# Layer 1's second product in seven block products instead of eight, with temporaries of several stages in shared buffers

## The chip, the cores and the metric

The kernel runs on one core of a Trainium2 chip. The metric is the time of one launch in device microseconds (us). Runs of one kernel on one chip agree within some 0.4%; every comparison is made with runs of the kernel before on the same chip in the same session.

## The reference, cut to what matters

Four graph layers follow one another on x of 128 batches x 128 nodes x 256 features, all in fp32. Each has a residual and a layer norm. The change touches layer 1:

```python
def _slconv(x, adj, S, W):
    support = jnp.einsum('bnf,fh->bnh', x, W)
    return jnp.einsum('nm,bmh->bnh', adj * S, support)

h = relu(_slconv(x, adj, S, W1))     # 256 -> 512
h = relu(_slconv(h, adj, S, W2))     # 512 -> 1024: the "second product"
return _slconv(h, adj, S, W3)        # 1024 -> 256
```

Layer 0 is attention over 512 edges (scores, a softmax by segments, a gather and a scatter through DRAM); layer 2 multiplies three mixed copies of x with three weights; layer 3 has two batch norms.

## The kernel before

A *quad* is a group of four batches; there are 32. Turn k of the loop works on several quads at once: layer 2 of quad k-1 (`stage_e`), the second product of quad k (`second`), values and queries of quad k+3 (`values_in`, `values`), the first part of layer 3 of quad k-1 (`stage_f`, `hidden`), the end of layer 0 for quad k+1 (`stage_a`), the third product of quad k, and the start of layer 1 for quad k+1 (`mix1`, `first`, `mix2`). An engine's instructions in the order of the source are called its *list* here, and in this case the order counts. Line numbers (L339) are those of the kernel; they shift by edits.

```python
def mix2(k, i):                       # mixing of the hidden features of batch i over the nodes
    pm = ps("pm2").rearrange("p (c n) -> p c n", n=N)
    for c in range(K1):               # K1 = 4
        nc.tensor.matmul(pm[:, c, :], s.h1[i][:, c * P:(c + 1) * P], wt_t, start=True, stop=True)
    nc.vector.tensor_copy(s.m2[:, :, i, :], pm)                                   # L330

def second(k, f):                     # f = 0..7, 128 of the 1024 outputs each
    ph = ps("ph2")
    for c in range(K1):
        nc.tensor.matmul(ph, w2_sb[:, c, f * P:(f + 1) * P],
                         s.m2[:, c].rearrange("p b n -> p (b n)"),
                         start=(c == 0), stop=(c == K1 - 1))                      # L339
    ...
    nc.scalar.activation(h.rearrange("p b n -> p (b n)"), ph, AF.Relu)            # L342

# in the loop; e is the quad two turns ahead, b the next one, g three ahead
    for f in range(K2):               # K2 = 8
        second(c, f)
        if first_one and f == 0:
            attention(b); scatter(b)
        if f % 2 == 0 and has_e:
            score(e, f // 2)          # three VectorE instructions, 3.65 us
        if f % 2 and has_b:
            by_row(b, f // 2)         # ScalarE copy of the scattered attention table
    if has_g and not first_one:
        values_in(g)                  # TensorE transposes x into pt, VectorE copies pt to xt
    if has_a:
        stage_f(a)                    # TensorE: pa
    ...                               # then values(g, 0): pq needs xt
```

## Time and profile before

| | before |
|---|---|
| median of three runs | 3413.97 us (3408.93 to 3415.3) |
| span of the profiled run, mean granted clock | 3411.7 us, 0.990 |
| TensorE busy | 98% |
| VectorE, ScalarE busy | 51%, 30% |
| one steady turn of the loop | 93.72 us |
| half-clock stretches in the steady turns | none |

The busy shares say which engine is full; the timeline says whether it ever waits; the view of waits adds up by line what TensorE waited for. In the kernel before that last view holds nothing in the loop above this line (what was waited for: us in total, times, longest):

```profile
PE po L294 <- DVE yt L288: 6.7, 28, 0.3
```

The rest of its list are waits of the start-up, the first turn and the end. "One steady turn" is here, and in all that follows, the time from the py product (in `stage_a`) of turn 1 to that of turn 28, divided by 27. Turns are counted from 0, the first turn.

### The profile page before, as it was taken

How to read it: one execution, taken by the hardware profiler on the slowest of the kernel's cores; microseconds unless marked ns; L12 is line 12 of the kernel's file. 1: busy time of each engine (PE TensorE's matmuls, PEld its weight loads, DVE VectorE, ACT ScalarE, POOL GpSimd, SP SyncE). 2: the span in 40 equal slices, each digit the busy share in tenths (PEclk: the TensorE clock that was granted, in tenths of full speed). 3: DMA queues.
4: the chain of work that ended last, by engine and by line, in shares of the span. 5: the costliest groups of instructions: out<-in, count | busy, mean ns of one | idle time of the engine just before them, and what ended most of it. 6: DMA issues, size and time to landing. Idle time of an engine off the chain costs nothing. (4 is left out here: it accounts for less than half of the span.)

```text
span 3411.7 us, 34420 instructions
## 1 busy us (share of the span) xinstructions
PE 3335.0 (98%) x13328; PEld 2109.5 (62%) x13328; DVE 1733.2 (51%) x3380; ACT 1014.8 (30%) x1750; POOL 636.8 (19%) x526
## 2 busy tenths in 40 slices
PE   6999999999999999999999999999999999999998
PEld 3566666666666666666666666666666666664444
DVE  6555455544554554455445555545554445224358
ACT  2222222222222222222222222222222222216438
POOL 5211112222221111122122211111222220000015
PEclk7999999999999999999999999999999999999999
DMA  7522233333333222333333333223333331015447
GB/s 232 165 83 74 76 93 100 99 99 87 99 90 90 89 76 71 93 100 99 100 87 99 96 85 91 77 68 92 100 99 99 87 99 38 19 38 197 158 152 258
DMA packets 120308, 346.01 MB, mean 101 GB/s; under 512 B 15056, under 2 KB 53328, under 8 KB 111824
## 3 DMA queue, kind: packets, MB, share of 16 engines
q0 software_dynamic: 45552, 151.55, 17.9%
q1 hardware_dynamic: 72544, 190.28, 15.6%
q8 instruction: 106, 1.74, 0.2%
q10 hardware_dynamic: 2048, 1.97, 0.2%
q14 instruction: 58, 0.48, 0.0%
HBM read 257.77 MB, written 85.98 MB: 101 GB/s over the span
## 5 line engine op out<-in xcount | busy, mean ns | idle before, releaser
L339 PE MATMUL ph<-m,w 128*128 128x512 f32 x2048 | 884.5, 592 | 1.4 <-DVE m L330 1.4
L339 PEld LDWEIGHTS ph<-m,w 128*128 128x128 f32 x2048 | 389.0, 190 | 477.3 <-issue 474.0
L205 POOL DMA_INDIRECT zs<-qd,src_idx x124 | 148.2, 1195 | 1718.3 <-DMA qd<-qt 1682.7
L352 PE MATMUL p<-w,h 128*128 128x256 f32 x2048 | 450.5, 381 | 0.0
L352 PEld LDWEIGHTS p<-w,h 128*128 128x128 f32 x2048 | 386.6, 190 | 53.0 <-issue 1.0
L400 PE MATMUL po<-l2w,ms 128*128 128x256 f32 x1536 | 347.5, 379 | 1.3 <-DVE ms L392 1.3
L342 ACT ACTIVATE h<-ph 128x512 f32<-128x512 f32 x256 | 152.7, 597 | 581.0 <-PE ph L339 581.0
L400 PEld LDWEIGHTS po<-l2w,ms 128*128 128x128 f32 x1536 | 284.3, 190 | 36.2 <-DVE ms L392 1.5
L319 PE MATMUL ph<-w,mx 128*128 128x512 f32 x512 | 235.8, 593 | 0.0
L189 PE MATMUL pq<-wqv,xt 128*128 128x512 f32 x512 | 228.6, 599 | 3.2 <-ACT xt L177 2.9
L440 PE MATMUL ph<-ag,l3w 128*128 128x512 f32 x512 | 225.4, 593 | 0.8 <-ACT ag L429 0.8
L205 POOL DMA_INDIRECT zs<-qd,dst_idx x124 | 194.3, 1567 | 144.0 <-DMA zs<-qd,src_idx 126.8
L365 DVE TENSOR_TENSOR xr<-xr,po 128x512 f32<-128x512 f32 x64 | 43.8, 684 | 340.5 <-PE po L363 340.4
L775 PE MATMUL po<-zl,l3w 128*128 128x512 f32 x496 | 213.0, 592 | 0.0
L261 POOL DMA_INDIRECT attd<-at,att_idx x128 | 127.6, 997 | 424.3 <-DMA attd<-at,att_idx 285.6
L119 DVE TENSOR_SCALAR xr<-xr,ln_mv,ln_rs 128x256 f32<-128x256 f32 x384 | 178.4, 507 | 6.9
L177 DVE COPY xt<-pt 128x512 f32<-128x512 f32 x56 | 36.1, 686 | 279.9 <-PE pt L175 279.9
L111 ACT ACTIVATE ln_sd<-ln_mv,eps 128x2 f32<-128x2 f32 x192 | 56.5, 294 | 397.4 <-DVE ln_mv L106 394.5
L440 PEld LDWEIGHTS ph<-ag,l3w 128*128 128x128 f32 x512 | 96.9, 190 | 122.1 <-issue 112.6
L775 PEld LDWEIGHTS po<-zl,l3w 128*128 128x128 f32 x496 | 94.2, 190 | 118.6 <-issue 115.3
L189 PEld LDWEIGHTS pq<-wqv,xt 128*128 128x128 f32 x512 | 96.0, 193 | 112.9 <-issue 108.7
L329 PEld LDWEIGHTS pm<-wt_t,h 128*128 128x128 f32 x1024 | 131.8, 191 | 47.4 <-issue 44.7
(188 smaller groups left out, 4121.0 us busy)
## 6 DMA issues: line engine op xcount, KB each, us to landing
ad<-attd SPq DMA_DIRECT2D x32, 1024.0 KB, 4.7
zd<-z SPq DMA_DIRECT2D x31, 1024.0 KB
zl<-zd SPq DMA_DIRECT2D x62, 512.0 KB, 4.4
xg<-in_x_dram SPq DMA_DIRECT2D x32, 512.0 KB, 6.6
xr<-in_x_dram SPq DMA_DIRECT2D x32, 512.0 KB
x3d<-xr SPq DMA_DIRECT2D x32, 512.0 KB, 2.9
x3l<-x3d SPq DMA_DIRECT2D x32, 512.0 KB, 4.7
out_dram<-x3l POOLq DMA_DIRECT2D x31, 512.0 KB
```

What stands on the lines that cost most here:

```text
L119: nc.vector.tensor_scalar(r[:, i, :], r[:, i, :], mv[:, i, 0:1], rs[:, i:i + 1], op0=ALU.subtract, op1=ALU.mult)
L189: nc.tensor.matmul(pq, s.xts[i // 2][:, i % 2, c, :], wqv[:, c, :], start=(c == 0), stop=(c == DC - 1))
L205: nc.gpsimd.indirect_dma_start(out=s.z[c], out_offset=None, in_=s.qd, in_offset=bass.IndirectOffsetOnAxis(ap=idx[:, c:c + 1], axis=0), com ...
L261: nc.gpsimd.indirect_dma_start(out=ad, out_offset=bass.IndirectOffsetOnAxis(ap=att_idx[:, c:c + 1], axis=0), in_=s.at[:, c, :], in_offset= ...
L319: nc.tensor.matmul(ph, s.mx[i // 2 * 2][:, i % 2, dc, :], w1_sb[:, dc, :], start=(dc == 0), stop=(dc == DC - 1))
L329: nc.tensor.matmul(pm[:, c, :], s.h1[i][:, c * P:(c + 1) * P], wt_t, start=True, stop=True)
L339: nc.tensor.matmul(ph, w2_sb[:, c, f * P:(f + 1) * P], s.m2[:, c].rearrange("p b n -> p (b n)"), start=(c == 0), stop=(c == K1 - 1))
L342: nc.scalar.activation(h.rearrange("p b n -> p (b n)"), ph, AF.Relu)
L352: nc.tensor.matmul(p3[:, t * D:(t + 1) * D], s.h2[f][:, j + t, :], w3_sb[:, f, :], start=(f == 0), stop=(f == K2 - 1))
L400: nc.tensor.matmul(po[:, i % 2, :], mss[i][:, t, dc, :], l2w[:, t, dc, :], start=(n3 == 0), stop=(n3 == 3 * DC - 1))
L440: nc.tensor.matmul(ph, l3w1[:, dc, c * P:(c + 1) * P], s.ag[:, dc, :], start=(dc == 0), stop=(dc == DC - 1))
L775: nc.tensor.matmul(po[o], w2t[:, c, o * P:(o + 1) * P], z[c // 2][:, c % 2, :], start=(c == 0), stop=(c == K3 - 1))
```

## The change

The second product is written as a product of 2 x 2 blocks: the 512 inputs and 1024 outputs of w2 in halves, and the four batches in two pairs. Strassen's scheme needs seven block products instead of eight, for sums of blocks beforehand and afterwards. GpSimd makes the sums of w2 once, at the start. VectorE makes those of m in `mix2`. The results are put together by accumulation in PSUM, by ScalarE copies of what is accumulated so far (`keep`) and by VectorE additions (`total`). As m and the sums take more room, the temporaries xt, yt, mx, h1, s3 and the copies share one ring of six buffers, and some loads move. The core of the diff:

```diff
@@ mix2
-            nc.vector.tensor_copy(s.m2[:, :, i, :], pm)
+            if i < 2:
+                nc.vector.tensor_copy(s.m2[:, B11:B21 + 1, :, i, :], pm)
+                return
+            nc.scalar.copy(m2[B22], pm[:, 1])                 # L347
+            nc.vector.tensor_sub(m2[T1], pm[:, 0], m2[B11])   # L348
+            nc.vector.tensor_sub(m2[T3], m2[B22], pm[:, 0])   # L349
+            nc.vector.tensor_sub(m2[T2], m2[B22], m2[T1])     # L350
+            nc.vector.tensor_sub(m2[T4], m2[B21], m2[T2])     # L351
@@ second: 14 half-products of 4 matmuls of 256 columns, after(i) runs what stands "between"
+            product(y, 0, "A11", B11)                         # L379
+            keep(p1, 0, "p1")                                 # L386, ScalarE
+            after(0)
+            product(z, 0, "S1", T1)
+            after(1)
... (eleven more half-products)
+            product(z, 1, "S4", B22)
+            total(1, 0, 1, z, u2)                             # L392, VectorE
+            relu(1, 0, 0)
+            relu(1, 0, 1)
+            after(13)
@@ the loop
+                between = {i: [] for i in range(14)}
+                if first_one:
+                    between[1] += [lambda: attention(b), lambda: scatter(b)]
+                if has_e:
+                    for c_, i in enumerate((0, 5, 9, 13)):
+                        between[i].append(lambda c_=c_: score(e, c_))
+                if has_b:
+                    for j, i in enumerate((3, 6, 10, 13)):
+                        between[i].append(lambda j=j: by_row(b, j))
+                second(c, between)
...
             steps = softmax_parts(e) if has_e else iter(())
-            next(steps, None)
... (shared buffers, GpSimd's sums and the moved loads are left out here)
```

More of the change, by code (lines that the diff above doesn't have):

```diff
@@ L128, in gnn_stack @@
         cst = phase.enter_context(tc.tile_pool(name="cst", bufs=1))
+        class Quad:
+            pass
+        quads = [Quad() for _ in range(NQ)]
         def cload(shape, name, ap, eng=None, dtype=F32, pool=cst):
@@ L135, in gnn_stack, with load_x @@
         ws = phase.enter_context(tc.tile_pool(name="ws", bufs=2))
-        def load_x(q, tag, bufs, pool=ws):
+        wk = phase.enter_context(tc.tile_pool(name="wk", bufs=2))
+        def load_x(q, tag="xr", bufs=3, pool=wk):
             t = pool.tile([P, QB, D], F32, tag=tag, name=f"{tag}{q}", bufs=bufs)
@@ L140, in load_x @@
             return t
-        xg0 = load_x(0, "xg", 2)
+        quads[0].xr = load_x(0)
         wqv = cload([P, DC, 2 * D], "wqv", w_qv_t.rearrange("(c p) f -> p c f", p=P))
@@ L157, in gnn_stack, with temp, values_in @@
         reset_b = ctile([R, E], "reset_b", pool=cst)
-        class Quad:
-            pass
-        quads = [Quad() for _ in range(NQ)]
-        def values_in(k, xg=None, copy=None):
+        def temp(name):
+            return wk.tile([P, 512], F32, tag="t", name=name, bufs=6)
+        def values_in(k, xg, copy=None):
             copy = copy or nc.vector.tensor_copy
@@ L169, in values_in @@
             s.xts = []
-            xg = load_x(k, "xg", 2) if xg is None else xg
             for j in range(0, QB, 2):
@@ L175, in values_in @@
                         nc.tensor.transpose(pt[:, t, c, :], xg[:, j + t, c * P:(c + 1) * P], ident)
-                xt = ws.tile([P, 2, DC, P], F32, tag="xt", name="xt")
+                xt = temp("xt").rearrange("p (b c n) -> p b c n", b=2, c=DC)
                 copy(xt, pt)
@@ L184, in values @@
             if i == 0:
-                s.qt = ws.tile([P, QB, D], F32, tag="qt", name=f"qt{k}", bufs=1)
+                s.qt = wk.tile([P, QB, D], F32, tag="xb", name=f"qt{k}", bufs=1)
                 s.xv = ws.tile([P, QB, D], F32, tag="xv", name=f"xv{k}", bufs=3)
@@ L286, in stage_a @@
                                              start=True, stop=True, tile_position=(0, h * DH))
-                yt = wk.tile([P, 2, DC, N], F32, tag="yt", name="yt")
+                yt = temp("yt").rearrange("p (b c n) -> p b c n", b=2, c=DC)
                 (nc.vector.tensor_copy if j else nc.scalar.copy)(yt, py)
@@ L306, in mix1 @@
                                      start=True, stop=True)
-            mx = wk.tile([P, 2, DC, N], F32, tag="mx", name="mx")
+            mx = temp("mx").rearrange("p (b c n) -> p b c n", b=2, c=DC)
             nc.scalar.copy(mx, pm)
@@ L311, in mix1 @@
                 s.h1 = {}
-                s.m2 = wk.tile([P, K1, QB, N], F32, tag="m2", name="m2", bufs=1)
+                s.m2 = m2_tile()
             s.mx[j] = mx
@@ L320, in first, with m2_tile @@
                                  start=(dc == 0), stop=(dc == DC - 1))
-            h1 = wk.tile([P, F1], F32, tag="h1", name="h1")
+            h1 = temp("h1")
             nc.scalar.activation(h1, ph, AF.Relu)
             s.h1[i] = h1
+        B11, B21, B22, T1, T2, T3, T4 = range(7)
+        def m2_tile():
+            return wk.tile([P, 7, 2, 2, N], F32, tag="m2", name="m2", bufs=1)
         def mix2(k, i):
             s = quads[k]
-            pm = ps("pm2").rearrange("p (c n) -> p c n", n=N)
+            pm = ps("pm2").rearrange("p (r c n) -> p r c n", r=2, n=N)
@@ L328, in mix2 @@
             for c in range(K1):
-                nc.tensor.matmul(pm[:, c, :], s.h1[i][:, c * P:(c + 1) * P], wt_t, start=True, stop=True)
-            nc.vector.tensor_copy(s.m2[:, :, i, :], pm)
-        def second(k, f):
-            s = quads[k]
-            if f == 0:
-                s.h2 = []
-            ph = ps("ph2")
-            for c in range(K1):
-                nc.tensor.matmul(ph, w2_sb[:, c, f * P:(f + 1) * P], s.m2[:, c].rearrange("p b n -> p (b n)"),
-                                 start=(c == 0), stop=(c == K1 - 1))
-            h = wk.tile([P, QB, N], F32, tag="h2", name="h2", bufs=K2)
-            nc.scalar.activation(h.rearrange("p b n -> p (b n)"), ph, AF.Relu)
-            s.h2.append(h)
+                nc.tensor.matmul(pm[:, c // 2, c % 2, :], s.h1[i][:, c * P:(c + 1) * P], wt_t, start=True, stop=True)
@@ new lines, in mix2, with second_sums @@
+            m2 = [s.m2[:, t, :, i % 2, :] for t in range(7)]
+            if i < 2:
[6 more added lines that the diff above has]
+            nc.vector.tensor_sub(m2[T4], m2[B21], m2[T2])
+        def second_sums():
+            a11, a12 = w2_sb[:, :2, :512], w2_sb[:, 2:, :512]
+            a21, a22 = w2_sb[:, :2, 512:], w2_sb[:, 2:, 512:]
+            s1, s2, s4 = (w2_s[:, i] for i in range(3))
+            nc.gpsimd.tensor_add(s1, a21, a22)
+            nc.gpsimd.tensor_sub(s2, s1, a11)
+            nc.gpsimd.tensor_sub(a21, a11, a21)
+            nc.gpsimd.tensor_sub(s4, a12, s2)
+            second.blocks = {"A11": a11, "A12": a12, "A22": a22, "S1": s1, "S2": s2, "S3": a21, "S4": s4}
@@ new lines, in second, with product, keep, block @@
+        def second(k, between):
+            s = quads[k]
+            s.h2 = [wk.tile([P, 2, QB, N], F32, tag="h2", name=f"h2_{g}", bufs=4) for g in range(4)]
+            y, z, x = [None] * 2, [None] * 2, [None] * 2
+            p1, u2, u3 = [None] * 2, [None] * 2, [None] * 2
+            def product(bank, g, blk_a, blk_b):
+                new = bank[g] is None
+                if new:
+                    bank[g] = ps("ph2").rearrange("p (i b n) -> p i b n", i=2, b=2)
+                wa = second.blocks[blk_a]
+                for i in range(2):
+                    f = (2 * g + i) * P
+                    for c in range(2):
+                        nc.tensor.matmul(bank[g][:, i].rearrange("p b n -> p (b n)"), wa[:, c, f:f + P],
+                                         s.m2[:, blk_b, c].rearrange("p b n -> p (b n)"),
+                                         start=new and i == 0 and c == 0, stop=i == 1 and c == 1,
+                                         skip_group_check=True)
+            def keep(to, g, name):
+                to[g] = temp(name).rearrange("p (i b n) -> p i b n", i=2, b=2)
+                nc.scalar.copy(to[g], y[g])
+            def block(g, row, col):
+                return s.h2[2 * row + g][:, :, 2 * col:2 * col + 2, :]
+            def total(g, row, col, bank, kept_):
+                nc.vector.tensor_add(block(g, row, col), bank[g], kept_[g])
+            def relu(g, row, col, src_=None):
+                h = block(g, row, col)
+                nc.scalar.activation(h, h if src_ is None else src_, AF.Relu)
+            def after(i):
+                for f in between.get(i, ()):
+                    f()
+            product(y, 0, "A11", B11)
[3 more added lines that the diff above has]
+            after(1)
+            product(y, 1, "A11", B11)
+            keep(p1, 1, "p1")
+            after(2)
+            product(y, 0, "S2", T2)
+            keep(u2, 0, "u2")
+            after(3)
+            product(x, 0, "A12", B21)
+            total(0, 0, 0, x, p1)
+            after(4)
+            product(y, 1, "S2", T2)
+            keep(u2, 1, "u2")
+            relu(0, 0, 0)
+            after(5)
+            product(y, 0, "S3", T3)
+            keep(u3, 0, "u3")
+            total(0, 1, 1, z, u3)
+            after(6)
+            product(z, 1, "S1", T1)
+            relu(0, 1, 1)
+            after(7)
+            product(y, 1, "S3", T3)
+            keep(u3, 1, "u3")
+            total(1, 1, 1, z, u3)
+            after(8)
+            product(y, 0, "A22", T4)
+            relu(0, 1, 0, y[0])
+            relu(1, 1, 1)
+            after(9)
+            product(z, 0, "S4", B22)
+            total(0, 0, 1, z, u2)
+            after(10)
+            product(y, 1, "A22", T4)
+            relu(1, 1, 0, y[1])
+            relu(0, 0, 1)
+            after(11)
+            product(x, 1, "A12", B21)
+            total(1, 0, 0, x, p1)
+            after(12)
+            product(z, 1, "S4", B22)
[3 more added lines that the diff above has]
+            after(13)
@@ L351, in third @@
                 for f in range(K2):
-                    nc.tensor.matmul(p3[:, t * D:(t + 1) * D], s.h2[f][:, j + t, :], w3_sb[:, f, :],
+                    nc.tensor.matmul(p3[:, t * D:(t + 1) * D], s.h2[f // 2][:, f % 2, j + t, :], w3_sb[:, f, :],
                                      start=(f == 0), stop=(f == K2 - 1))
-            s3 = wk.tile([P, 2 * D], F32, tag="s3", name="s3")
+            s3 = temp("s3")
             nc.scalar.copy(s3, p3)
@@ L382, in mix @@
                 nonlocal pt
-                ms = wk.tile([P, 3, DC, N], F32, tag="ms", name="ms")
+                ms = wk.tile([P, 3 * DC * N], F32, tag="ms", name="ms").rearrange("p (k c n) -> p k c n", k=3, c=DC)
                 pm = ps("pm3").rearrange("p (c k n) -> p c k n", c=DC, k=2)
@@ L420, in stage_f @@
             s = quads[k]
-            ag = wk.tile([P, DC, QB * N], F32, tag="ag", name="ag", bufs=1)
+            ag = [wk.tile([P, 3 * DC * N], F32, tag="ms", name="ag")[:, :QB * N] for _ in range(DC)]
             pas = [ps("pa") for _ in range(DC)]
@@ L428, in stage_f @@
                 if dc == 0:
-                    nc.scalar.copy(ag[:, dc, :], pa)
+                    nc.scalar.copy(ag[dc], pa)
                 else:
-                    nc.vector.tensor_copy(ag[:, dc, :], pa)
+                    nc.vector.tensor_copy(ag[dc], pa)
             s.ag = ag
@@ L439, in hidden @@
             for dc in range(DC):
-                nc.tensor.matmul(ph, l3w1[:, dc, c * P:(c + 1) * P], s.ag[:, dc, :],
+                nc.tensor.matmul(ph, l3w1[:, dc, c * P:(c + 1) * P], s.ag[dc],
                                  start=(dc == 0), stop=(dc == DC - 1))
@@ L452, in gnn_stack @@
         cst2 = phase.enter_context(tc.tile_pool(name="cst2", bufs=1))
-        wk = phase.enter_context(tc.tile_pool(name="wk", bufs=2))
         wo = ctile([P, DC, D], "wo", pool=cst2)
@@ L456, in gnn_stack @@
         w2_sb = ctile([P, K1, F2], "w2", pool=cst2)
+        w2_s = ctile([P, 3, 2, F2 // 2], "w2_s", pool=cst2)
         w3_sb = ctile([P, K2, D], "w3", pool=cst2)
@@ L460, in gnn_stack @@
         l3w1 = ctile([P, DC, F3], "l3w1", pool=cst2)
+        halves_left = []
         def scratch(name, dtype=F32):
-            return wk.tile([P, E], dtype, tag="h2", name=name, bufs=K2)
+            if not halves_left:
+                t = wk.tile([P, 2, E], F32, tag="h2", name=name, bufs=4)
+                halves_left.extend((t[:, 1], t[:, 0]))
+            t = halves_left.pop()
+            return t if dtype == F32 else t.bitcast(dtype)
         def iteration(k):
@@ L469, in iteration @@
             first_one = k == 0
-            if has_b:
-                quads[b].xr = load_x(b, "xr", 3, wk)
+            if has_b and b > 2:
+                quads[b].xr = load_x(b)
             if has_a:
@@ L474, in iteration @@
             if has_c:
-                for f in range(K2):
-                    second(c, f)
-                    if first_one and f == 0:
-                        attention(b)
-                        scatter(b)
-                    if f % 2 == 0 and has_e:
-                        score(e, f // 2)
-                    if f % 2 and has_b:
-                        by_row(b, f // 2)
+                between = {i: [] for i in range(14)}
[8 more added lines that the diff above has]
+                second(c, between)
             if has_g and not first_one:
-                values_in(g)
+                values_in(g, quads[g].xg)
+                if g + 1 < NQ:
+                    quads[g + 1].xg = load_x(g + 1, "xg", 1, ws)
             if has_a:
@@ L543, in start @@
                            allow_small_or_imprecise_dtypes=True)
-            zero = wk.tile([P, N * R], F32, tag="m2", name="zero", bufs=1)
+            zero = m2_tile().rearrange("p t c b n -> p (t c b n)")[:, :N * R]
             nc.gpsimd.memset(zero, 0.0)
@@ L560, in start @@
                                         accum_out=rank[:, c:c + 1])
-            perm = w2_sb[:, :2, :].rearrange("p c f -> p (c f)").rearrange("p (c e) -> p c e", c=NE)
+            perm = w2_s.rearrange("p t c f -> p (t c) f")[:, :NE, :]
             for c in range(NE):
@@ L569, in start @@
                                              in_offset=bass.IndirectOffsetOnAxis(ap=adj_idx[:, c:c + 1], axis=0))
-            xg1 = load_x(1, "xg", 2)
+            quads[1].xr = load_x(1)
             nc.sync.dma_start(att_dram[0][:N * N, :].rearrange("(t s) r -> t (s r)", s=N), zero)
             nc.sync.dma_start(wo, w_out_t.rearrange("(c p) f -> p c f", p=P))
-            values_in(0, xg0, nc.scalar.copy)
+            values_in(0, quads[0].xr, nc.scalar.copy)
             for i in range(QB):
                 values(0, i, nc.scalar.copy, nc.scalar)
-            xg2 = load_x(2, "xg", 2)
+            quads[2].xr = load_x(2)
             def sorted_columns(t):
@@ L595, in start @@
             nc.scalar.copy(src_row[:R, :], pr[:R, :])
-            values_in(1, xg1, nc.scalar.copy)
+            values_in(1, quads[1].xr, nc.scalar.copy)
             for i in range(QB):
@@ L600, in start @@
             z2 = zpool.tile([P, 2, QB * D], F32, tag="z", name="z_1", bufs=1)
-            gather(1, [z2[:, 0, :], z2[:, 1, :], wk.tile([P, QB * D], F32, tag="xb", name="xb_1", bufs=1),
-                       wk.tile([P, QB * D], F32, tag="ag", name="ag_1", bufs=1)])
+            gather(1, [z2[:, 0, :], z2[:, 1, :], w2t.rearrange("p c d -> p (c d)"),
+                       l3w1.rearrange("p c f -> p (c f)")])
             pair_row = scratch("pair_row")
@@ L628, in start @@
                 nc.vector.tensor_scalar(rs, kp, 1.0, BIG, op0=ALU.subtract, op1=ALU.mult)
-            xg3 = load_x(3, "xg", 2)
-            quads[0].xr = load_x(0, "xr", 3, wk)
+            xg3 = load_x(3, "xg", 1, ws)
             for c in range(NE):
@@ L640, in start @@
                 next(steps)
-            values_in(2, xg2, nc.scalar.copy)
+            values_in(2, quads[2].xr, nc.scalar.copy)
             next(steps)
@@ L656, in start @@
             nc.sync.dma_start(bias, bass.AP(tensor=l2_bias.tensor, offset=l2_bias.offset, ap=[[0, P], [1, D]]))
-            nc.sync.dma_start(l3w1, l3_w1_t.rearrange("(c p) f -> p c f", p=P))
-            nc.sync.dma_start(w2t, l3_w2_t.rearrange("(c p) f -> p c f", p=P))
             for t, vecs in ((bn1, (l3_b1, l3_g1, l3_be1)), (bn2, (l3_b2, l3_g2, l3_be2))):
@@ L695, in start @@
             gather(2)
+            second_sums()
             for c in range(NE - 1):
@@ L701, in start @@
             values_in(3, xg3, nc.scalar.copy)
+            quads[4].xg = load_x(4, "xg", 1, ws)
             for i in range(QB):
@@ L704, in start @@
             score(1, NE - 1)
+            nc.sync.dma_start(l3w1, l3_w1_t.rearrange("(c p) f -> p c f", p=P))
+            nc.sync.dma_start(w2t, l3_w2_t.rearrange("(c p) f -> p c f", p=P))
             mix1(0, 0)
```

## The prediction

> **What bounds the kernel now.** I read the page first, for the engine that is full.
>
> ```profile
> PE 3335.0 (98%) x13328; PEld 2109.5 (62%) x13328; DVE 1733.2 (51%) x3380; ACT 1014.8 (30%) x1750; POOL 636.8 (19%) x526
> ...
> L339 PE MATMUL ph<-m,w 128*128 128x512 f32 x2048 | 884.5, 592 | 1.4 <-DVE m L330 1.4
> ...
> L352 PE MATMUL p<-w,h 128*128 128x256 f32 x2048 | 450.5, 381 | 0.0
> ```
>
> TensorE is busy 98% of the span and almost never waits. L339 is the product to be changed: 32 quads (groups of four batches) of 32 matmuls, each recorded twice, 26% of the span. L352 is the same kind of stream at 256 columns, and gives the price of the new pieces.
>
> Then the timeline of TensorE over one steady turn of the loop (93.7 us from one L339 block to the next, 196.98 to 290.70):
>
> ```profile
> 184.45 2.76 PE L400 MATMUL po<-l2w,ms 128*128 128x256 f32 x12
> ...
> 196.98 27.63 PE L339 MATMUL ph<-m,w 128*128 128x512 f32 x64
> 224.45 1.04 PE L175 MATMUL pt<-ident,xg 128*128 128x128 f32 x8
> 225.32 1.95 PE L425 MATMUL pa<-ahat_t,xr 128*128 128x128 f32 x16
> 227.11 0.60 PE L227 MATMUL pe<-ident,es 128*16 128x128 f32 x4
> 227.54 7.03 PE L189 MATMUL pq<-wqv,xt 128*128 128x512 f32 x16
> ```
>
> Columns: start, length, engine, line. Starts follow one another without a gap. So each saved TensorE microsecond is worth one, and so is each new wait, unless other engines keep up. What VectorE did meanwhile:
>
> ```profile
> 182.48 0.69 DVE L330 COPY m<-pm 128x512 f32<-128x512 f32 x1 [0.32 <-PE pm L329]
> 183.57 0.42 DVE L392 TENSOR_TENSOR ms<-pt,diag_bc 128x256 f32<-128x256 f32 x1 [0.39 <-PE pt L391]
> ...
> 211.10 1.22 DVE L215 SCALAR_TENSOR_TENSOR zs<-zs 128x1024 f32<-128x1024 f32 x1
> 212.35 1.23 DVE L217 TENSOR_TENSOR zs<-zs,a_bc 128x1024 f32<-128x1024 f32 x1
> 213.61 1.22 DVE L218 TENSOR_REDUCE es<-zs 128x16 f32<-128x1024 f32 x1
> 214.87 0.22 DVE L220 TENSOR_TENSOR es<-es,log_col 128x64 f32<-128x64 f32 x1
> 225.08 1.29 DVE L177 COPY xt<-pt 128x512 f32<-128x512 f32 x2 [9.99 <-PE pt L175]
> ```
>
> The four scores (three instructions, 3.65 us each) ended 10 us before L339 did; VectorE stood waiting when TensorE made pt, and had xt ready for pq. That slack is what the change spends.
>
> Last, a gap of middle size in the first turn, and the granted clock around it (windows in us, length, TensorE busy and instructions, clock):
>
> ```profile
> 148.51 5.27 PE L294 MATMUL po<-wo,yt 128*128 128x256 f32 x16 [2.52 <-ACT yt L288]
> ```
>
> ```profile
> 147.00:149.00 2.00, 0.49 (x1) 0.82 1.03 197
> 149.00:150.00 1.00, 1.00 (x4) 0.50 1.03 205
> 150.00:151.00 1.00, 1.00 (x4) 0.50 0.29 53
> 151.00:152.00 1.00, 1.00 (x5) 0.66 0.08 16
> ```
>
> A wait of 2.52 us was followed by about 3.4 us at half clock: those 16 matmuls took 5.2 us from start to next start, against 3.45 at L352's pace. It costs a second time, 1.7 us.
>
> [...]0.2175 us per L352 record (64 in 13.92 us) against 0.429 per L339 record (64 in 27.47). [...]the trace has 0.68 to 0.69 us for 128x512 and 0.42 for 128x256. [...]xv on VectorE starts only after ScalarE's qt from the same bank (105.6 us of such idle time).
>
> **The change, part by part.** The order of instructions in the built kernel decides the rest[...].
>
> 1. *TensorE work.* 14 half-products of 4 matmuls, two records each: 112 records x 0.2175 = 24.36 us against 27.47. Saved: 3.11 us per turn; weight loads of 0.19 us still hide beneath 0.2175. Without waits, 32 x 3.11 = 99.5 us, 2.9%.
>
> 2. *ScalarE* gets 6 copies of 0.59 and 2 of 0.37 per turn, 4.3 us, against 70% idle. By my table each copy is done over 1 us before TensorE adds into its bank again. Free in the steady turns.
>
> 3. *VectorE* gets 8 additions of 0.69 us among the scores, and 8 subtractions of 128x256 for two 128x512 copies. On average it has room (51% busy). At two places the order has none.
>
> *End of the product.* Time 0 is its start. Layer norm leaves VectorE at 3.2 us as before, and the scores now stand at positions 0, 5, 9 and 13 of 14. The last half-product ends at 24.36; its addition starts at about 24.6 and ends at 25.25; only then comes the last score (3.65), the log addition and the first xt copy, which ends at about 29.7. TensorE goes on with pt (0.87) and pa (1.79) until 27.0, and then pq needs xt. Wait: 2.7 us. It swallows nearly all of the 3.11. Moving pe behind two pq takes pe's need for es off, not pq's need for xt. This holds for loop turns 1 to 28 (of 0 to 32), 28 x 2.7 = 76 us. Turn 29 has no pq, and pe waits for es: 3 us. Turns 30 and 31 have no scores and keep their gain.
>
> *After the second mixing.* Before, m of batch 3 was copied by 183.2 and the product ms by 184.0, ready for L400 at 184.45. Now batch 2 first has a ScalarE copy from the same bank (from 181.47 for 0.37), then four subtractions, which follow at some 0.34 us, or 0.45 where one needs its neighbour: about 1.47 us. Two batches end at 184.8, ms at 185.25, and L400 starts 0.8 us late. 31 x 0.8 = 25 us.
>
> 4. *First turn.* ScalarE's by-row copy waits there for the table scattered through DRAM:
>
> ```profile
> 136.93 1.06 ACT L271 COPY adc<-ad 128x512 f32<-128x512 f32 x1 [13.27 <-DMA ad<-attd]
> ```
>
> Before, free banks let TensorE run on to 143.46. Now the copy of u2 for the second half stands behind it in ScalarE's list, and half-product 8 needs that bank. It can start at about 139 instead of 128; six half-products (10.4 us), a half-clock stretch (1.7) and the score chain (4.75 behind the last half-product, with no pt or pa to cover it) give pe at about 156 instead of 143.5: +12 us, its own saving included.
>
> 5. *Clock.* Windows of the trace before that were 27 to 37% active were followed by half clock, some at 53 to 65% were not. A 2.7 us gap leaves a window below about 45% if the window holds 1.9 us of it; with windows at random phase that is (2.7 - 1.9) + (3.4 - 1.9) = 2.3 of 3.4 us, some 70%. Each costs about 1.6 us. An estimate: 29 x 0.7 x 1.6 = 32 us.
>
> 6. *Shared buffers, moved loads, GpSimd's four sums* (two to three us each by L374's 1.28 us for 512 columns, hidden in the start-up). By the rotation of the six shared temporaries every slot's last reader is long done. Zero, give or take 4 us.
>
> Sum: -31 x 3.11 + 76 + 3 + 25 + 12 + 32 = +52 us.
>
> **Rivals.** (a) *The saving comes through*, 3414 - 99 = 3315 us. For it: 98% busy TensorE and idle VectorE in the averages. Against: it needs xt in time, and VectorE's list puts 4.5 us of work between the last half-product and xt, against 2.66 us of cover. (b) *Waits but no clock loss*: +20 us, 3434. For it: [...]a 1.94 us gap near the end of the loop kept full clock. Against: the 2.52 us gap above. (c) *Clock lost in every turn and a longer wait after the mixing* (1.1 us): +75 us, 3489. (d) *TensorE waits inside the product for its six banks*: y's reuse is 1.0 us or more behind its copies; if one came late by 1 us per turn, +30 us.
>
> **Range and chances.** I take 3460, a little under the sum's 3466, because the clock term is the weakest. (b) and (c), with some room for errors in my table, give 3418 to 3500. The limit for slower is 3482, within reach if the clock falls in nearly every turn: 0.30. Faster than 3346 needs an error in the order of VectorE's work: 0.04.
>
> **What would show it.** Right: the groups of the new product have a mean busy near 0.22 us; pq waits for VectorE's xt about 28 times, about 2.7 us each; L400 waits for ms 31 times, under 1.1 us; the granted clock falls to half behind some of the pq waits; the first product has one wait near 10 us for ScalarE. Wrong: no wait of pq (step 3), waits inside the product (step 2), a clock of 0.99 throughout (step 5), or matmuls of 256 columns well above 0.2175 us (step 1).

The 0.68 to 0.69 and the 0.42 us are those of VectorE's fp32 tensor_tensor instructions (L365 and L404, L392); step 5's windows are stretches of the length that the half clock took in the first turn, 3.4 us.

## The result, and the profile after

The kernel after is correct and took 3485.91 us in median (3483.71 to 3489.39, four runs), the kernel before 3411.45 us beside it. The ratio is 1.0218, with a 95% interval of 1.0201 to 1.0236. A ratio is the mean time of one kernel's fast runs over that of the other's of the same rounds, so it isn't quite the ratio of the medians quoted. The time lies in the predicted range, 26 us above the predicted 3460, and just past the limit of 2% that the prediction had thought the less likely side.

TensorE has less work and more idle time. The first line is from the page, the next two are the groups of the new product:

```profile
PE 3278.7 (94%) x14864; PEld 2415.0 (69%) x14864; DVE 1871.8 (54%) x3764; ACT 1141.2 (33%) x2006; POOL 634.4 (18%) x530
...
L379 PE MATMUL ph<-m,w 128*128 128x256 f32 x2048 | 476.5, 381 | 11.7 <-ACT u L386 11.7
...
L379 PE MATMUL ph<-m,w_s 128*128 128x256 f32 x1536 | 362.9, 379 | 0.8 <-DVE m L348 0.8
```

Busy time fell by 3335.0 - 3278.7 = 56.3 us, though some of what is left ran at half clock; idle time rose by 132 us, and that makes the 76 us of the span. The view of waits has where:

```profile
PE pq L192 <- DVE xt L180: 73.6, 28, 2.6
PE pe L230 <- DVE es L223: 22.8, 4, 10.6
PE po L297 <- DVE yt L291: 22.1, 24, 1.0
PE po L506 <- DVE ms L498: 21.4, 32, 1.3
PE ph L379 <- ACT u L386: 11.7, 1, 11.7
```

Columns: who waited, for what, us in total, times, longest us. The first of these in the timeline of TensorE, at the end of the product in turn 1:

```profile
242.97 1.04 PE L178 MATMUL pt<-ident,xg 128*128 128x128 f32 x8
243.84 1.95 PE L531 MATMUL pa<-ahat_t,xr 128*128 128x128 f32 x16
248.42 5.09 PE L192 MATMUL pq<-wqv,xt 128*128 128x512 f32 x8 [2.63 <-DVE xt L180]
```

and VectorE's list over the same stretch shows why:

```profile
243.17 0.69 DVE L392 TENSOR_TENSOR h<-ph,u 128x512 f32<-128x512 f32 x1 [1.03 <-PE ph L379]
243.78 1.22 DVE L218 SCALAR_TENSOR_TENSOR zs<-zs 128x1024 f32<-128x1024 f32 x1
...
247.54 0.22 DVE L223 TENSOR_TENSOR es<-es,log_col 128x64 f32<-128x64 f32 x1
247.69 1.28 DVE L180 COPY xt<-pt 128x512 f32<-128x512 f32 x2
```

The last addition waits for the last half-product, the last score stands behind the addition, and xt behind the score. The pt transposes were done at 244; xt came at 248.3. The eight pq records then took 5.09 us from first start to last end; without a clock loss they take 3.70 (a turn near 1594 us). The granted clock is the column behind the busy times (windows, length, busy us and instructions of PE, PEld, DVE, ACT and POOL, clock, DMA share, GB/s):

```profile
245.00:247.00 2.00, 0.79 (x8) 0.60 (x6) 1.94 (x2) 1.02 (x2) 0.00 (x0) 1.00 0.92 218
247.00:249.00 2.00, 0.58 (x1) 0.50 (x2) 1.97 (x5) 0.00 (x0) 0.00 (x0) 0.71 0.13 45
249.00:251.00 2.00, 2.00 (x3) 0.67 (x2) 0.56 (x1) 0.00 (x0) 0.00 (x0) 0.50 0.03 8
```

The trace also has the clock's own record of changes. From turn 1 to turn 29 of the loop it has 16 half-clock stretches, each 3.413 us long or twice that, together 68.3 us, which is 34 us of lost work. In the kernel before there is none. Below, a *window* is the time between two marks that are set 3.413 us apart through the starts of these stretches.

The other end of the turn is the second mixing, with ms 0.65 us late for L506:

```profile
205.35 0.43 DVE L351 TENSOR_TENSOR m<-m 128x256 f32<-128x256 f32 x1
205.69 0.75 DVE L498 TENSOR_TENSOR ms<-pt,diag_bc 128x256 f32<-128x256 f32 x2
```

```profile
206.16 2.86 PE L506 MATMUL po<-l2w,ms 128*128 128x256 f32 x12 [0.65 <-DVE ms L498]
```

Cut into stretches by the starts of py, the 76.0 us are: +22.8 up to the py of turn 1 (241.37 to 264.18), +56.2 in 27 steady turns (93.72 to 95.80 us each), and -3.0 behind the py of turn 28, where there is no pq from turn 29 on and no score from turn 30 on.

A steady turn adds up so, in us: product -3.30 (27.47 to 24.17); pq +2.63; ms +0.65; yt +0.55, which is (22.1 - 6.7) / 28; clock +1.14, which is half of the 61.4 us at half clock between the two marks, over 27. TensorE's first records behind each of two waits took 0.1 us longer than otherwise (L506's twelve 2.86 for 2.76, L192's eight 3.70 for 3.60): +0.2. Sum +1.87 of the measured +2.08.

### The profile page after: what moved, and what is told of

Its sections match the earlier page's. It is cut to its first block, busy times and chain, and to the rows that moved or that the text cites. A ratio compares the mean times of both kernels' runs of the same rounds, so it can differ in the third digit from the quotient of the medians.

```text
span 3487.7 us, 38188 instructions
## 1 busy us (share of the span) xinstructions
PE 3278.7 (94%) x14864; PEld 2415.0 (69%) x14864; DVE 1871.8 (54%) x3764; ACT 1141.2 (33%) x2006; POOL 634.4 (18%) x530
## 3 DMA queue, kind: packets, MB, share of 16 engines
q10 hardware_dynamic: 2048, 1.97, 0.2%
## 5 line engine op out<-in xcount | busy, mean ns | idle before, releaser
L379 PE MATMUL ph<-m,w 128*128 128x256 f32 x2048 | 476.5, 381 | 11.7 <-ACT u L386 11.7
L208 POOL DMA_INDIRECT zs<-qd,src_idx x124 | 136.4, 1100 | 1817.1 <-DVE e L239 1560.8
L379 PEld LDWEIGHTS ph<-m,w 128*128 128x128 f32 x2048 | 390.9, 191 | 65.7 <-ACT u L386 12.1
L506 PE MATMUL po<-l2w,ms 128*128 128x256 f32 x1536 | 350.7, 381 | 21.4 <-DVE ms L498 21.4
L379 PE MATMUL ph<-m,w_s 128*128 128x256 f32 x1536 | 362.9, 379 | 0.8 <-DVE m L348 0.8
L192 PE MATMUL pq<-wqv,xt 128*128 128x512 f32 x512 | 265.7, 668 | 76.9 <-DVE xt L180 73.6
L506 PEld LDWEIGHTS po<-l2w,ms 128*128 128x128 f32 x1536 | 284.2, 190 | 63.7 <-DVE ms L498 29.0
L379 PEld LDWEIGHTS ph<-m,w_s 128*128 128x128 f32 x1536 | 291.8, 190 | 40.8 <-issue 1.2
L192 PEld LDWEIGHTS pq<-wqv,xt 128*128 128x128 f32 x512 | 104.8, 215 | 195.8 <-issue 112.1
L392 DVE TENSOR_TENSOR h<-ph,u 128x512 f32<-128x512 f32 x128 | 87.9, 686 | 138.4 <-ACT u L386 101.1
```

Source lines behind the costliest of these rows:

```text
L192: nc.tensor.matmul(pq, s.xts[i // 2][:, i % 2, c, :], wqv[:, c, :], start=(c == 0), stop=(c == DC - 1))
L208: nc.gpsimd.indirect_dma_start(out=s.z[c], out_offset=None, in_=s.qd, in_offset=bass.IndirectOffsetOnAxis(ap=idx[:, c:c + 1], axis=0), com ...
L379: nc.tensor.matmul(bank[g][:, i].rearrange("p b n -> p (b n)"), wa[:, c, f:f + P], s.m2[:, blk_b, c].rearrange("p b n -> p (b n)"), start= ...
L392: nc.vector.tensor_add(block(g, row, col), bank[g], kept_[g])
L506: nc.tensor.matmul(po[:, i % 2, :], mss[i][:, t, dc, :], l2w[:, t, dc, :], start=(n3 == 0), stop=(n3 == 3 * DC - 1))
```

## The experiments

All twelve were correct (the labels skip e4; the record has no such run). "Half clock" below is the total length of the half-clock stretches from turn 1 to turn 29, "yt" what po waited for the second yt copy, "ms" what layer 2's product waited for ms (1.3 us of it stands in the last turn, in every kernel).

| run | ratio to before | median, us | turn, us | pq waits, us | ms waits, us | yt waits, us | half clock, us |
|---|---|---|---|---|---|---|---|
| before, first profile | 1 | 3411.45 | 93.72 | 0 | 1.3 | 6.7 | 0 |
| after, first profile | 1.0218 | 3485.91 | 95.80 | 73.6 | 21.4 | 22.1 | 68.3 |
| e1_scores_early | 0.9842 | 3343.25 | 90.84 | 0 | 21.5 | 0.6 | 0 |
| e2_fill_gap | 1.0101 | 3430.14 | 93.73 | 0 | 21.5 | 0.6 | 0 |
| e3_defer | 1.0072 | 3422.33 | 93.51 | 73.6 | 1.3 | 0.6 | 47.8 |
| e5_yt_scalar | 1.0222 | 3470.93 | 95.30 | 73.6 | 21.5 | 1.2 | 85.3 |
| e6_first_turn | 1.0154 | 3470.50 | 95.72 | 73.6 | 21.4 | 22.6 | 58.0 |
| e7_old_product | 1.0037 | 3430.20 | 94.33 | 0 | 1.3 | 23.0 | 0 |
| e8_sums_late | 1.0185 | 3476.99 | 95.56 | 73.6 | 21.4 | 21.2 | 44.4 |
| e9_all | 0.9726 | 3325.42 | 91.04 | 0 | 1.3 | 17.8 | 0 |
| before_again | one look | 3399.28 | 93.21 | 0 | 1.3 | not listed | 0 |
| after_again | 1.0214 | 3470.47 | 95.30 | 73.6 | 21.4 | 0.6 | 92.2 |
| e7b_softmax_back | 1.0006 | 3399.57 | 93.21 | 0 | 1.3 | not listed | 0 |
| e10_all_hide | 0.9696 | 3293.69 | 89.93 | 0 | 1.3 | 0.3 | 0 |

e1, e2, e3 and e5 ran one after another on one chip, which is called a session here, e6 to e9 in a second, the last four in a third; the two first profiles are older. The column "yt" goes by session before it goes by edit: in the first and third sessions there is hardly any such wait in any kernel, in the others it is 17 to 23 us for every kernel with the later softmax step. I call these sessions *prompt* and *late*. That came out only with the last runs; some of the expectations below were written without knowing it.

### e1: the last score off the end

```diff
-                    for c_, i in enumerate((0, 5, 9, 13)):
+                    for c_, i in enumerate((0, 5, 9, 13) if first_one else (0, 0, 6, 9)):
```

> Edit: from the second turn of the loop on, the four scores stand at positions 0, 0, 6 and 9 of the 14 half-products instead of 0, 5, 9 and 13; nothing else moves. Theory (the last score between the last addition and the xt copy makes pq wait, and the wait costs a second time through the clock): the 28 pq waits of 2.63 us (73.6 us) go to under 3 us in all, the half-clock stretches of the loop go with them (pq busy from 265.7 us back to about 229), time about 3486 - 71 - 36 = 3379 us, ratio to the kernel before about 0.990. Rival 1 (the wait only moves, to pe, to an addition that a bank waits for, or to yt): time falls by less than 40 us, to 3446 or more, and the waits stand under another line. Rival 2 (the clock falls for another reason than this gap): waits gone, but pq or its neighbours still at half clock in about 17 turns, time about 3412.

The ratio fell from 1.0214 (the kernel after in another prompt session) to 0.9842: 3.7%, or 126 us. The pq waits are gone and so are all half-clock stretches. TensorE goes from pa to pq without a pause:

```profile
242.84 1.95 PE L531 MATMUL pa<-ahat_t,xr 128*128 128x128 f32 x16
244.63 3.60 PE L192 MATMUL pq<-wqv,xt 128*128 128x512 f32 x8
```

This is more than the expected 0.990, because I had counted the clock by the first profile (34 us). In a prompt session the kernel after loses 92.2 / 2 = 46 us by it: 73.6 + 46 + 28 x 0.1 = 122 us. The comparison doesn't hang on the other session: e5, run beside e1 with an edit that had no effect there, is at 1.0222. Both rivals fall: no wait took the place of this one, and the half clock went with the gap. Moving the scores up, the last by four positions, makes the change a gain of 1.6%.

### e2: the gap filled with idle matmuls

```diff
             pq = ps("pq")
+            if i == 0 and k > 3:
+                for _ in range(3):
+                    nc.tensor.matmul(pq, wqv[:, 0, :P], wqv[:, 1, :], start=True, stop=True)
```

> Edit: in the turns that have pq, three idle matmuls of 512 columns (six records, some 2.6 us at L192's pace) are put ahead of the first pq matmul, into the same bank, which the first real matmul overwrites; VectorE's order and its lateness stay. Theory (of the loss, some 36 us is the clock alone, set off by TensorE standing still): the idle time in front of pq becomes busy time of equal length, under 10 us of waits are left in front of pq, no half-clock stretch is left in the steady turns, the real pq matmuls are back at 1.7 us per four, and the time falls by 30 to 40 us to about 3450 (ratio about 1.011). Rival (clock falls in these turns for another reason, or costs nothing): time within 8 us of 3486, half-clock stretches as before in about 17 turns.

The first real matmul overwrites what the idle ones left in the bank: the result of e2 is correct. VectorE is as late as ever, but TensorE has something to do:

```profile
243.20 2.74 PE L193 MATMUL pq<-wqv 128*128 128x512 f32 x6
245.99 3.70 PE L195 MATMUL pq<-wqv,xt 128*128 128x512 f32 x8
```

No half-clock stretch is left in the steady turns, and the ratio is 1.0101 instead of 1.0214, 38 us less, in the expected 30 to 40. So matmuls whose result nobody uses save time here. The wait costs its own length (73.6 us), which e2 still pays, and the clock costs more than half as much again (38 us by the ratios, 46 by the stretches), separately. In the kernel after the two looked like one loss.

### e3: half of the subtractions later

```diff
@@ mix2
-            nc.vector.tensor_sub(m2[T2], m2[B22], m2[T1])
-            nc.vector.tensor_sub(m2[T4], m2[B21], m2[T2])
@@ stage_e, behind mix(0) and mix(1)
+            if k + 1 < NQ:
+                mix2_rest(k + 1)     # T2 and T4, both batches in one instruction each
```

> Edit: the subtractions T2 and T4, which the product needs only from its fourth half-product on, leave the second mixing and are done once per turn for both batches (2 of 128x512 instead of 4 of 128x256), in VectorE's list behind the ms products of batches 0 and 1. Theory (the eight subtractions make ms late): L506's 32 waits of about 0.65 us (21.4 us) fall to under 3 us, time down by some 20 us to about 3466, give or take 8 because a changed length of the turn shifts where the clock's windows fall. Rival (L506 waits for something else, such as ScalarE's copies for ms): the wait stays above 0.4 us per turn and is put down to ScalarE.

The waits of L506 (here L509) fell to 1.3 us, as expected. The group that had waited 0.65 us (206.16 in the kernel after) now starts without a wait:

```profile
201.05 2.76 PE L509 MATMUL po<-l2w,ms 128*128 128x256 f32 x12
```

The time fell by far more than the expected 20, give or take 8: 1.0214 to 1.0072 is 48 us. The rest is the clock: 47.8 us at half clock against 92.2 in after_again, so 22 us less lost; 20 + 22 and 0.1 us of restart for each of 31 waits make 45. The expectation had allowed 8 us for what a shorter turn does to the clock, and it was 22; the section on the clock below has the reason.

### e5: ScalarE copies both yt

```diff
-                (nc.vector.tensor_copy if j else nc.scalar.copy)(yt, py)
+                nc.scalar.copy(yt, py)
```

> Edit: ScalarE copies both yt instead of the first only. In the kernel after, VectorE's yt copy starts 2.1 us behind the end of py in 23 turns, each time just where GpSimd's issue of a gather ends, and 0.1 us behind it in the turns where no such issue lies across the end of py. Theory (VectorE's copy cannot start while GpSimd issues this gather): ScalarE's copy starts within 0.7 us of the end of py in nearly all turns, the 22.1 us of waits of po for yt fall to under 3 us, time down by some 15 to 22 us to about 3467. Rival 1 (py's completion reaches other engines late, whatever engine waits): ScalarE's copy starts 2 us late as well, the waits stay near 22 us. Rival 2 (the shared temporary slots make it wait): the same, as the slots stay the same.

The waits fell to 1.2 us, which looked like the theory. It was none: on that chip at that time yt is prompt with VectorE too (0.6 us in e1, e2 and e3), so the run tells nothing of what makes it late. The ratio stayed at 1.0222, the half clock at 85.3 us. An experiment whose effect is already absent in its neighbours of the same session is no experiment.

### e6: the first turn

```diff
-                    for c_, i in enumerate((0, 5, 9, 13)):
+                    for c_, i in enumerate((1, 5, 9, 13) if first_one else (0, 5, 9, 13)):
-                    for j, i in enumerate((3, 6, 10, 13)):
+                    for j, i in enumerate((13,) * 4 if first_one else (3, 6, 10, 13)):
```

> Edit: in the first turn only, attention and scatter stand before the first score in VectorE's list (score at position 1, behind them), and all four by-row copies stand at the end of ScalarE's list for the product. Theory (the stall of the first turn is the u2 copy standing behind a by-row copy that waits for the scattered table, which itself is late because the score stands ahead of attention): the 11.7 us wait of the product for ScalarE goes, the scattered table lands about 3 us earlier (near 141.5 instead of 144.8), pe starts near 150 instead of 164.7, time down by 12 to 18 us to about 3471. Rival (the scattered table is needed anyway for stage A right behind): the product runs on, but py waits for adc about as long, time down by less than 5 us.

In the kernel after the first turn stalled here:

```profile
144.79 1.05 ACT L274 COPY adc<-ad 128x512 f32<-128x512 f32 x1 [16.32 <-DMA ad<-attd]
```

```profile
146.38 6.61 PE L379 MATMUL ph<-m,w 128*128 128x256 f32 x16 [11.68 <-ACT u L386]
```

With the by-row copies at the end, the wait of L379 for ScalarE is gone from the list, pe starts at 147.86 instead of 164.67, and py at 148.80 instead of 165.61:

```profile
148.80 2.85 PE L288 MATMUL py<-adc,xv 128*64 128x128 f32 x32
```

The ratio fell from 1.0218 to 1.0154: 22 us, more than the expected 12 to 18, of which 17 are the first turn; the half clock of the steady turns is 10 us shorter, which is 5 more. The rival, that py would wait as long, falls.

### e7 and e7b: all but Strassen

e7 has the eight block products and the single copy of m again, no GpSimd sums, and everything else of the change. e7b also puts the first softmax step back where it was:

```diff
             steps = softmax_parts(e) if has_e else iter(())
+            next(steps, None)
             for i in range(QB):
```

> Edit: Strassen undone (eight block products, 512 columns, one copy of m per batch, no sums on GpSimd), everything else of the change kept: the shared temporaries, the ring of xr and xg, the later loads, the later softmax step. Theory (these parts cost nothing in the steady turns): within 6 us of the kernel before, 3406 to 3418, ratio 0.998 to 1.002; L506 waits near 1 us in all, po for yt near 7 us in all, no half clock in the steady turns. Rival (shared buffers add waits, part of the 15 us at yt among them): ratio 1.004 or more, with yt waits near 22 us.

> Edit: as e7 (eight block products, all else of the change kept), and the first softmax step put back ahead of the four pq, as in the kernel before; what is left of the change is the shared temporaries, the rings and the loads. Theory (e7's 0.37% came from the later softmax step, which shifts GpSimd's gathers against py and so yt's start): po's wait for yt falls from 23.0 us to about 7, ratio 0.998 to 1.002. Rival (the shared temporaries or the loads cost it): ratio 1.003 or more and yt waits as in e7.

e7 came out at 1.0037, outside the expected 0.998 to 1.002, with yt waits of 23.0 us in its late session, against 6.7 us in the kernel before in an older late one. e7b came out at 1.0006, but in a prompt session, where yt doesn't wait anyway. So shared temporaries, rings and moved loads cost nothing that a prompt session shows (0.9993 to 1.0020). In a late session the parts besides Strassen cost about 0.4%, some 13 us. The waits at yt, 16 us longer than in the kernel before's older profile, would account for it, but no profile of the kernel before was taken in e7's session; whether the softmax step or the shared ring does it was not separated either, since e7b and e7 fell into different kinds of session.

### e8: GpSimd's sums later

```diff
+            nc.gpsimd.tensor_copy(att_late, quads[1].es[:, NE - 1, :1])
+            second_sums()            # here, behind the last score of quad 1, not ahead of it
```

> Edit: GpSimd's four sums of weights start only when the last score of batch group 1 is done (a one-column copy of that score's result stands ahead of them). Theory (GpSimd's sums slowed the two VectorE instructions of that score from 1.22 to 2.31 and 3.25 us): both are back at 1.2 to 1.3 us, the wait of pe of 4.48 us falls by about 3 us to some 1.4, and the product of turn 0 starts about 3 us earlier unless it now waits for the sums; time down by 0 to 4 us. Rival (they were slow for another reason, such as the DMA traffic of the gathers): both stay above 2 us.

In the start-up of the kernel after, a VectorE score and GpSimd's sums (POOL) ran at once:

```profile
100.60 2.31 DVE L218 SCALAR_TENSOR_TENSOR l3w<-l3w 128x1024 f32<-128x1024 f32 x1
101.78 3.33 POOL L361 TENSOR_TENSOR w_s<-w,w_s 128x1024 f32<-128x1024 f32 x1
102.94 3.25 DVE L220 TENSOR_TENSOR l3w<-l3w,a_bc 128x1024 f32<-128x1024 f32 x1
```

In e8 the first of the two took 1.22 us, and the second:

```profile
100.80 1.23 DVE L220 TENSOR_TENSOR l3w<-l3w,a_bc 128x1024 f32<-128x1024 f32 x1
```

and pe waited 1.37 us instead of 4.48. The theory holds, but the slowness moved on with the sums: a scan (L235) then took 2.01 us instead of 1.20. The times of the kernel after: L220 began at 102.94 and ended 1.08 us behind the end of L361 at 105.11, and L361, which had begun while L218 ran, took 3.33 us where the sum ahead of it took 2.35. In e8 the sum L360 began at 108.49, while the scan ran, and took 3.28 us. What in the chip makes them slow each other the runs don't show. My prediction had called the sums hidden. The time fell by more than the expected 0 to 4 us (1.0218 to 1.0185, 11 us), and the excess may again be the clock: 44.4 us at half clock instead of 68.3 is 12 us. That is the profiled run, though, the fastest of five that lie between 3473 and 3487 us; how much of the 11 us is the cure itself is not shown.

### e9: all five cures

> Edit: the cures of e1, e3, e5, e6 and e8 together (in the first turn the scores stand at 1, 1, 6, 9). Theory (the five losses are separate and add up): from 3486 take 74 for pq, 36 for the clock, 20 for ms, 20 for yt, 15 for the first turn and 3 for the sums: about 3318 us, 3310 to 3335, ratio 0.973, faster than both kernels; TensorE over 98% busy again. Rival (the work on VectorE only moves and something else waits instead): above 3350.

The ratio is 0.9726, as expected: 2.7% faster than the kernel before, 4.8% faster than the kernel after. One wait stayed, and it brought down my theory of yt. Here ScalarE copies both yt, and in this late session it was late as VectorE had been:

```profile
235.23 1.97 PE L288 MATMUL py<-adc,xv 128*64 128x128 f32 x32
...
236.54 0.59 ACT L291 COPY yt<-py 128x512 f32<-128x512 f32 x1 [0.61 <-PE py L288]
...
239.47 0.59 ACT L291 COPY yt<-py 128x512 f32<-128x512 f32 x1 [2.35 <-PE po L297]
```

The second copy waits for py's last matmul only. That ended at 237.20; the copy began 2.27 us later. The view names po as its releaser because the update of TensorE's semaphore that py's last matmul makes is recorded at 239.45 in this trace, just ahead of po's at 239.54. The theory's other mark, TensorE over 98% busy, was missed too: it is 97%.

### before_again and after_again

> Edit: none, the kernel before once more, for its profile on the same chip as the three runs beside it. In the earlier runs the lateness of yt went by the chip session and not by the edit: in the session of e1, e2, e3 and e5 the second yt copy starts 2.05 us behind the start of py in nearly all turns, in that of e6 to e9 4.06 to 4.25 us, and in e9 it is ScalarE that is late there[...]. If the session is all, po waits for yt in the kernel before as long as in the kernel after on this chip (both near 22 us or both near 1). If the order of the later softmax step counts as well, the kernel before has about 7 us where after has 22.

> Edit: none, the kernel after once more beside the kernel before on this chip. Ratio near 1.022 if this chip shows the late yt as the first one did, near 1.017 if not (15 of 3414 us less); pq waits 73.6 us and L506 waits 21.4 us as before in either case.

In this prompt session the second yt copy starts 2.01 us behind the start of py in the kernel before (3.39 in the older profile) and 2.05 in the kernel after (4.08). The kernel is the same and the lateness isn't, so it is of the session. The pq and L506 waits are 73.6 and 21.4 us again. The ratio, however, is 1.0214 and not the 1.017 that I expected without yt's 15 us: the half clock takes 92.2 us here instead of 68.3, which gives 12 of the 15 back.

### e10: the third product between the po halves

```diff
             for j in range(0, QB, 2):
+                if j and mid:
+                    mid()            # third(c, 0): 7 us of TensorE work
                 po = ps("po")
```

> Edit: e9, and the first half of the third product (32 records, 7 us of TensorE work that needs neither yt nor po) put between the two po halves. Theory (whatever makes yt late, 7 us of other work hides it): po's waits for yt fall from 17.8 us plus 5.8 us to under 3, ratio some 0.006 below e9's 0.9726 if this chip shows the late yt, 0.965 to 0.970; nothing else gets longer. Rival (layer norm of the second half comes later and mixing has to wait for it): a new wait of pm for xr, ratio 0.973 or more.

The ratio is 0.9696 (0.9682 to 0.9709), 3293.69 us beside 3397.38: the fastest kernel, and no new wait appeared. Its turn of 89.93 us is 3.28 below the 93.21 of before_again, which is the 3.30 us of the product almost in full. The session was prompt, so that the 7 us hide a late yt was not tested. Nor is it shown that e10 is faster than e9 for its edit: e9 was not run in a prompt session, and its waits for yt (17.8 us, and 5.8 that the view puts down to issue) are more than the 0.3% between the two ratios.

TensorE is busy 98% of the span again, with 3219.3 us of work instead of 3325.4 in before_again.

### The clock, from all the runs together

In the clock records, the half-clock stretches start at whole multiples of 3.413 us from one another, in every run. In after_again 24 of the 26 distances between neighbours are 95.57 us, 28.00 windows, and two are 187.73, 55.00 windows. A turn without a loss takes about 93.7 us there (95.30, less half of the 85.3 us at half clock between the marks over 27 turns); a turn with one takes 1.7 us more, 95.4, which is close to 28 windows. So a hit turn puts the next gap at nearly the same place in its window, about 0.15 us earlier, and the loss repeats: 27 stretches, 26 of them behind pq gaps. In the first profile of after the turns without a loss were longer by the late yt, and most distances are 191.15 us, 56 windows: every second turn was hit. In e3 the turn was shorter, and most distances are 82 or 55 windows, every third or second turn. No run set out to shift the phase alone, but the traces settle that the phase decides. Six runs have the pq gap of 2.63 us, 28 times each. Take marks 3.413 us apart through the starts of a run's stretches: the 105 gaps that begin at most 0.66 us ahead of a mark or at most 1.44 us behind one were all followed by half clock (12 of the 28 in e3 and in e8, 26 in after_again), and the 63 that begin 1.44 to 2.71 us behind one were not. In other words, the window between two marks had to hold 1.97 us of this gap.

## Why the prediction was right, and where it was not

The bottleneck, the main wait and the loss in front were right, and the time was in the range. By its steps:

1. *TensorE work.* Predicted -3.11 us per turn, measured -3.30: a half-product of eight records takes 1.726 us, 0.2158 per record, while the 0.2175 from L352 included a tail. Rival (d), waits inside the product, did not occur in a steady turn.
2. *ScalarE free.* Right in the steady turns.
3. *End of the product.* Predicted 2.7 us, 28 times, 76 us; measured 2.63, 28 times, 73.6. e1 shows that the order of VectorE's list is the cause. *After the second mixing*: predicted 0.8 us, measured 0.65; e3 shows that the subtractions are the cause.
4. *First turn.* Mis-sized. The term says +12 us; measured +21.6 up to the py of that turn (143.99 to 165.61). Three things were left out: GpSimd's sums delayed pe of the start-up by 3.7 us (107.84 for 104.19; e8), the score now stands ahead of attention in VectorE's list, so that the by-row copy could start at 144.79 and not at the 136.93 that the step took over from the kernel before, and the stall was long enough for 13.7 us at half clock instead of one window. e6 shows that 17 us of it go by the order alone.
5. *Clock.* Predicted 32 us from 20 stretches of 1.6; measured 68.3 / 2 = 34 us, from 16 stretches, four of them two windows long. Its core was right: it let a window fall when it holds 1.9 us of the gap, and the traces put that at 1.97; 105 of 168 gaps, 63%, were hit, for the 70% of the step. What failed is the phase taken as random from turn to turn: it follows from the turn before, so that the same kernel lost 34 us in one session and 46 in another. That 34 came so close to 32 is in part luck. The step's reading of busy shares doesn't hold either: in the kernel before, the window from 62.89 to 66.30 us, with TensorE busy for 1.82 us of 3.41 (53%), was followed by half clock. e1 and e2 show that the gap sets it off, which rival (b) had denied.
6. *Shared buffers, loads, sums.* Zero was right in a prompt session (e7b). In a late session yt waits were not foreseen: 22.1 - 6.7 = 15 us. The sums were not hidden.

From the prediction's own sum of 3466 to 3486, by these terms: first turn +10, yt +15, restarts behind the waits +6 (0.2 in 28 turns), clock +2, pq -2, mixing -5 (20 for 25), product -6 (32 x 0.19): +20. The 3460 had been set 6 below that sum, which is the rest of the 26. It is luck that no more is left: +33 of terms left out or too small stand against -13 of terms too large, and the 15 of yt belong to the session.

Left open: what delays the signal of py in some sessions. It isn't the engine that waits: the packed traces record the update of TensorE's semaphore by py's last matmul 2.08 us behind its end in the first profile of after and 2.21 in e9 (medians of 27 turns), 1.40 in that of the kernel before, and 0.02 in all runs of the prompt sessions. VectorE is out (e9 has ScalarE late). It isn't the place of GpSimd's gathers alone: relative to py they stand the same in e1, where yt is prompt, and in the first profile of after, where it is late. It isn't the product (e7 has it). It isn't the change, since the kernel before has it.

## What to carry to other kernels

When TensorE is full, a saving there is only as good as the last instruction of another engine that stands between the shortened work and the next: list that engine's instructions behind the last piece, and move out of its way whatever can be done earlier (here scores of 3.65 us each, which turned +2.1% into -1.6%). The gaps of 2.52 and 2.63 us on TensorE here cost their length and, where they fell badly (105 of the 168 of 2.63 us), a window of 3.413 us at half clock, 1.7 us of work; with useless matmuls in those of 2.63 us (e2) no half clock was left in the steady turns, and the time was 38 us less. Useful work in that place was not tried. Read an experiment by its waits and by its clock, against a run of the same session: here the clock gave or took back 10 to 25 us in e3, e8 and after_again, in runs whose edit had nothing to do with it.
